# Features of five blocks: rows normed on ScalarE and turned by way of DRAM and VectorE

## The chip, the cores and the metric

The kernel runs on one core of one Trainium2 chip. Times are device microseconds of one execution, as median of the runs shown. A profile is one execution, recorded instruction by instruction; "us" in its timelines counts from its first instruction. The engines have short names there: PE is TensorE, PEld its weight loads, DVE is VectorE, ACT is ScalarE, POOL is GpSimd, SP is SyncE, which here only issues DMAs (SPq).

## The reference, cut to what matters

The kernel computes one layer: a graph step over a dense 4096x4096 adjacency matrix, then attention and a mixture of experts. The change concerns the graph step alone.

```python
def _layernorm(x, axis=-1, eps=1e-5):
    m = jnp.mean(x, axis=axis, keepdims=True)
    v = jnp.var(x, axis=axis, keepdims=True)
    return (x - m) / jnp.sqrt(v + eps)

def _L0_gnn_ref(features, adj, neigh_W, lin_W):
    h = features @ neigh_W.T
    deg = adj.sum(axis=1, keepdims=True) + 1.0
    h = adj @ h / deg
    z = jnp.concatenate([features, h], axis=-1) @ lin_W.T
    return z

# x is 4096 x 256, adj 4096 x 4096, float32
x = x + _L0_gnn_ref(_layernorm(x, axis=-1), adj, L0_gnn_neigh_W, L0_gnn_lin_W)
...
```

## The kernel before

**Tiles.** The 4096 rows of x are eight blocks of 512, each held as `res[b]`: 128 partitions, four row tiles `t`, 256 columns. The adjacency matrix is 8x8 blocks of 512x512, 1 MB each, that stream through three buffers; `load(n)` asks for the next but two as soon as a block is done with. One row of eight such blocks is an aggregation, `aggregate(b)`; each block is multiplied in seven products on halves of it (a Strassen scheme) with the normed rows `g[jb]`. `halve(n)` makes the sums of the adjacency block's halves, `halve_x(b)` those of the rows. The part of lin_W that meets the features themselves does not go through the adjacency matrix: `features(b)` multiplies block b's normed rows, with the columns on the partitions, and adds the product to `res[b]`.

**What happens to one block of x.** `scales_x(b)`: mean and variance on VectorE (L159, L161), then on GpSimd the power -1/2 (L165, L166) into `rstd[b]`. `normed_x(b, t)` (L451): VectorE writes (x - mean) * rstd into `g[b]`, four instructions a block. `turned_x(b)` (L437, L439): TensorE transposes `g[b]` in eight 128x128 pieces and ScalarE copies the result into `turned[b]`. `features(b)` (L509, L514): sixteen matmul passes on TensorE and two adds on VectorE; it also norms block b+1. `halve_x(b)` (L463 to L470): one small copy on ScalarE, four operations on VectorE.

**Order.** The schedule is written out by hand: each engine takes its instructions in the order in which the program names them, and semaphores hold an instruction until what it reads is there. Row 0 of the aggregation has all the work on x in it, some blocks ahead. In its step `jb`, after four of the seven products, come `halve(jb + 1)`, `features(jb + 2)`, `halve_x(jb + 2)` and `scales_x(jb + 4)`; at the step's end `turned_x(jb + 3)`, and then the next adjacency load. Step 0 also has `turned_x(2)`, directly after `halve(1)`. Blocks 0 and 1 are done ahead of the loop, and so are the statistics of blocks 2 and 3. Step 3 has `load_rest`, seven DMAs for the attention's weights.

**The other use of the way through DRAM.** From row 1 on, `qkv(b - 1)` handles the finished block b - 1. It norms its rows into `kT[b]` and `vv[b]`, whose own contents come later, with the columns in the order of `in_order`; `leave` (L599) writes them in two DMAs to a scratch tensor in DRAM, `turning`; `fetch` (L611) reads them back in four DMAs, so that each 32x32 square stands with its 32 rows on 32 partitions; `turn` (L621) has VectorE transpose all squares in two instructions. There are two scratch tensors, used in turns.

Of the kernel before, what the change touches and what calls it, by code (L numbers as in the profile page):

```python
# [9 lines left out]
F32 = mybir.dt.float32  # L10
I32 = mybir.dt.int32
SP = mybir.EngineType.SP
AF = mybir.ActivationFunctionType
ALU = mybir.AluOpType
# [3 lines left out]
P = 128  # L18
N = 4096
C = 256  # L20
NB = 8
TB = 4
# [9 lines left out]
Q = HD // 2  # L32
# [34 lines left out]
def fast_kernel(  # L67
# [24 lines left out]
    nc = tc.nc  # L92
# [27 lines left out]
    for e in range(NE):  # L120
# [16 lines left out]
    res = [  # L137
        res_all[:, b * TB * C : (b + 1) * TB * C].rearrange("p (t c) -> p t c", t=TB)
        for b in range(NB)
    ]  # L140
    qT_all = const.tile([P, NB * 2 * 512], F32, name="qT_all")
    qT = [
        qT_all[:, b * 1024 : (b + 1) * 1024].rearrange("p (c i) -> p c i", c=2)
        for b in range(NB)
    ]
    mv = [const.tile([P, TB, 2], F32, name=f"mv{b}") for b in range(NB)]
# [42 lines left out]
    def in_order(x):  # L189
        return x.rearrange("p (g c d) -> p c g d", g=4, c=2)  # L190

    def in_groups(x):
        return x.rearrange("p (c g d) -> p c g d", g=4, c=2)
# [65 lines left out]
    with (  # L259
# [179 lines left out]
                nc.scalar.copy(dst[:, :, cols], tr.rearrange("p c t i -> p c (t i)"))  # L439

        turned = {}

        def scales_x(b, at_a_time=TB):
            for t in range(0, TB, at_a_time):
                some = slice(t, t + at_a_time)
                stats(gx, b, range(TB)[some])
                power(rstd[b][:, some], mv[b][:, some, 1:2], 1.0, EPS_LN)

        def normed_x(b, t):
            i = t // 2 * 2  # L450
            nc.vector.tensor_scalar(  # L451
                g[b][:, i : i + 2, t % 2, :], res[b][:, t, :].rearrange("p (h c) -> p h c", h=2),
                mv[b][:, t, 0:1], rstd[b][:, t], op0=ALU.subtract, op1=ALU.mult,
            )

        def turned_x(b):

            turned[b] = qT[b % 4]
            transposed(lambda t, c: g[b][:, t // 2 * 2 + c, t % 2, :], turned[b])
# [39 lines left out]
            halves_of[n] = m  # L499
        def features(b):  # L500
            fT = turned.pop(b)
            for t in range(TB if b + 1 < NB else 0):
                normed_x(b + 1, t)
            for h in range(2):
                pj = p_pj.tile([P, 2, C], F32, tag="pj", name=f"pf_{b}_{h}")
                for t in range(2):
                    for c in range(2):
                        at = (2 * h + t) * P
                        nc.tensor.matmul(  # L509
                            pj[:, t, :], fT[:, c, at : at + P], l1_sb[:, c, :],  # L510
                            start=(c == 0), stop=(c == 1),
                        )
                x1 = res[b][:, 2 * h : 2 * h + 2, :]
                nc.vector.tensor_add(x1, x1, pj)  # L514
# [52 lines left out]
                ),  # L567
            )

        turning = [tc.dram_tile([512, C], F32, name=f"turning{n}") for n in range(2)]  # L570
        last_z = gs.tile([P, 1024], F32, name="last_z")

        def qkv(b):

            made = {}

            def scales():
                stats(gx, b)
                var = mv[b][:, :, 1:2]
                power(both[b], var, *BOTH)  # L580
                power(rstd[b], var, 1.0, EPS_LN)

            def norm():

                made["h0"] = [
                    t.rearrange("p (t c) -> p t c", t=2)
                    for t in (kT[b], vv[b].rearrange("p t c -> p (t c)"))
                ]
                for t in range(TB):
                    nc.vector.tensor_scalar(  # L590
                        in_order(made["h0"][t // 2][:, t % 2, :]), in_groups(res[b][:, t, :]),
                        mv[b][:, t, 0:1], both[b][:, t], op0=ALU.subtract, op1=ALU.mult,
                    )
                made["ratio"] = ratio(gx, b)

            def leave():

                for n, h0 in enumerate(made.pop("h0")):
                    nc.sync.dma_start(  # L599
                        turning[b % 2][n * 2 * P : (n + 1) * 2 * P].rearrange(  # L600
                            "(t p) c -> p t c", p=P
                        ),
                        h0,
                    )

            def fetch():

                made["z"] = qT_all[:, (b + 1) * 1024 : (b + 2) * 1024] if b + 2 < NB else last_z
                squares = turning[b % 2].rearrange("(m i) (g e) -> g i m e", i=Q, g=4)
                for n in range(4):  # L610
                    nc.sync.dma_start(  # L611
                        made["z"][n * Q : (n + 1) * Q].rearrange("p (m e) -> p m e", e=2 * Q),
                        squares[n],
                    )

            def turn():

                made["hT"] = qT[b]
                z = made.pop("z").rearrange("p (m c d) -> p c m d", c=2, d=Q)
                for c in range(2):  # L620
                    nc.vector.transpose(  # L621
                        qT[b][:, c, :].rearrange("p (m i) -> p m i", i=Q), z[:, c]
                    )

            def values_and_logits():
                for h in range(2):
                    pj = p_tr.tile([P, 2, 2, P], F32, tag="tr", name=f"pv_{b}_{h}")
                    pj = pj.rearrange("p c t i -> p c (t i)")
                    for i in range(2):
                        at = (2 * h + i) * P  # L630
                        for c in range(2):
                            nc.tensor.matmul(  # L632
                                pj[:, i, 0 : NE + P], made["hT"][:, c, at : at + P],
                                wqkv_sb[:, c, QK:], start=(c == 0), stop=(c == 1),
                            )
                    nc.scalar.copy(vv[b][:, 2 * h : 2 * h + 2, :], pj[:, :, NE : NE + P])  # L636
                    for i in range(2):
                        t = 2 * h + i
                        nc.scalar.activation(
                            first_lg[b][:, t, :], pj[:, i, 0:NE], AF.Copy,  # L640
                            scale=made["ratio"][:, t],
                        )

            def turned_heads(ms):
                pjs = [p_pj.tile([P, 512], F32, tag="pj", name=f"pq_{b}_{m}") for m in ms]
                for m, pj in zip(ms, pjs):
                    for c in range(2):
                        nc.tensor.matmul(
                            pj, wqkv_sb[:, c, m * P : (m + 1) * P], made["hT"][:, c, :],
                            start=(c == 0), stop=(c == 1),  # L650
                        )
                for m, pj in zip(ms, pjs):
                    to = kT[b] if m == 2 else qT[b][:, m, :]
                    rot = gx.tile([P, 512], F32, tag="rot", name=f"rot_{b}_{m}", bufs=1)
                    nc.vector.tensor_mul(to, pj, tables[b][:, 0, :])  # L655
                    for n in range(4):
                        nc.scalar.activation(  # L657
                            rot[n * Q : (n + 1) * Q, :], pj[(n ^ 1) * Q : ((n ^ 1) + 1) * Q, :],
                            AF.Copy, scale=1.0 if n % 2 else -1.0,
                        )  # L660
                    nc.gpsimd.tensor_mul(rot, rot, tables[b][:, 1, :])  # L661
                    nc.gpsimd.tensor_add(to, to, rot)

            return [
                [scales, lambda: turn_tables(b)], [norm, leave], [],
                [values_and_logits, lambda: turned_heads((2,))], [lambda: turned_heads((0, 1))],
            ], {
                (2, "end"): [fetch], (2, "loaded"): [lambda: spread_tables(b)],
                (3, "end"): [turn],
            }  # L670
# [23 lines left out]
        features(1)  # L694
        halve_x(1)
        scales_x(3)
        steps = {jb: [] for jb in range(NB)}
        for jb in range(NB):
            for f, b in (
                (halve, jb + 1), (features, jb + 2), (halve_x, jb + 2), (scales_x, jb + 4),  # L700
            ):
                if b < NB or f is halve:
                    steps[jb].append(lambda f=f, b=b: f(b))
            if jb + 3 < NB:
                steps[jb, "end"] = [lambda b=jb + 3: turned_x(b)]
        steps[0].insert(1, lambda: turned_x(2))
        steps[3].append(load_rest)
        for jb, f in ((5, scale_rest), (6, bounds), (6, turn_wo), (7, router_wo)):
# [2 lines left out]
        for b in range(NB):  # L711
            if b:

                steps = {0: behind, (0, "end"): at_end}
# [2102 lines left out]
```

## Time and profile before

| | |
|---|---|
| median of three runs | 1514.38 us (1513.91 to 1514.47) |
| the profiled execution's own time | 1513.4 us |
| its span, first to last instruction | 1511.7 us |
| row 0 of the aggregation, TensorE's first to last matmul in it | 18.7 to about 96 us |
| HBM read and written | 188.15 MB and 30.80 MB |

Busy time in five stretches of the part that matters; columns are the length, then for each engine the busy us and the number of its instructions, the granted TensorE clock, the busy share of the DMA engines and the GB/s that they moved:

```profile
20.00:24.00 4.00, 3.76 (x22) 3.17 (x21) 3.97 (x11) 1.17 (x3) 0.16 (x1) 1.00 1.02 370
24.00:28.00 4.00, 4.00 (x20) 3.54 (x19) 3.90 (x13) 0.00 (x0) 1.53 (x2) 1.00 0.18 54
28.00:32.00 4.00, 4.00 (x24) 3.46 (x23) 3.97 (x10) 1.21 (x3) 0.46 (x1) 1.00 0.25 61
32.00:36.00 4.00, 4.00 (x21) 3.51 (x20) 3.83 (x13) 0.00 (x0) 1.23 (x2) 1.00 0.48 201
36.00:40.00 4.00, 4.00 (x20) 3.51 (x19) 4.00 (x9) 0.00 (x0) 0.77 (x1) 1.00 0.00 0
```

The engines are TensorE, its weight loads, VectorE, ScalarE and GpSimd, in this order. TensorE is busy in all of each stretch but the first, where it waited 0.24 us for a copy by ScalarE; VectorE is hardly less busy; ScalarE has some 1.2 us of work in 8 to 10 us. A busy TensorE is not one at its peak, because the ends of its matmuls are modelled.

### The profile page before, as it was taken

The numbers are of one execution on the slowest core, as the hardware profiler recorded it, in microseconds if no ns is written. First come the engines' busy times: TensorE is split into PE (matmuls) and PEld (weight loads), VectorE is DVE, ScalarE is ACT, GpSimd is POOL, SyncE is SP. The second block draws the span as 40 slices with busy tenths as digits, with TensorE's granted clock in tenths as the row PEclk, the third lists the DMA queues.
The fourth block names the chain that finished last, engine by engine and source line by source line (L and its number), as shares of the span: only waits on it lengthen the run. The fifth ranks groups of instructions, "written<-read, shape, count | busy, mean of one in ns | idle before, by whom it ended". The sixth has DMA issues, their size and how long they took to land. (4 is left out here: it accounts for less than half of the span.)

```text
span 1511.7 us, 28589 instructions
## 1 busy us (share of the span) xinstructions
PE 1498.3 (99%) x10739; PEld 1103.8 (73%) x10739; DVE 1082.8 (72%) x2237; ACT 545.3 (36%) x977; POOL 564.1 (37%) x649
## 2 busy tenths in 40 slices
PE   9999999999999999999999999999999999999997
PEld 7888888888888544444444444358899999999996
DVE  7855665656765577779879879795676877777872
ACT  2102011021020455655656655653222343343341
POOL 2102122121221331364564653551523464554542
PEclk9999999999999999999999999999999999999999
DMA  6435645555556000011010110029977898999965
GB/s 243 133 119 182 193 151 177 168 168 166 165 183 184 5 1 16 29 50 39 30 59 24 38 43 30 29 77 331 260 182 217 261 272 236 269 270 247 271 157 135
DMA packets 124365, 219.51 MB, mean 145 GB/s; under 512 B 77402, under 2 KB 100698, under 8 KB 110586
## 3 DMA queue, kind: packets, MB, share of 16 engines
q1 hardware_dynamic: 110682, 199.35, 41.5%
q0 software_dynamic: 12720, 17.47, 6.4%
q8 instruction: 86, 1.41, 0.4%
q10 hardware_dynamic: 816, 0.79, 0.2%
q14 instruction: 61, 0.50, 0.1%
HBM read 188.15 MB, written 30.80 MB: 145 GB/s over the span
## 5 line engine op out<-in xcount | busy, mean ns | idle before, releaser
L826 PE MATMUL sc<-qT_all,kT 64*64 64x512 f32 (+3 forms) x2304 | 282.2, 557 | 0.5 <-ACT pt_all L834 0.3
L538 PE MATMUL acc<-a,g 128*128 128x256 f32 x1024 | 244.0, 379 | 0.0
L538 PEld LDWEIGHTS acc<-a,g 128*128 128x128 f32 x1024 | 194.1, 190 | 32.1 <-issue 6.7
L826 PEld LDWEIGHTS sc<-qT_all,kT 64*64 64x64 f32 x2304 | 91.2, 133 | 128.5 <-issue 109.4
L834 ACT ACTIVATE pt_all<-sc 128x1024 f32<-128x1024 f32 (+3 forms) x157 | 148.7, 954 | 96.8 <-PE sc L826 91.8
L1908 POOL DMA_INDIRECT acc_dram<-y,late x40 | 63.0, 1575 | 176.6 <-ACT y L1897 113.2
L538 PE MATMUL acc<-more_sums,g 128*128 128x256 f32 x512 | 126.3, 379 | 0.0
L854 DVE TENSOR_TENSOR late<-late,pt_all 128x1024 f32<-128x1024 f32 (+3 forms) x91 | 106.8, 1173 | 24.3 <-POOL pt_all L836 9.6
L538 PEld LDWEIGHTS acc<-more_sums,g 128*128 128x128 f32 x512 | 97.2, 190 | 13.1
L868 PE MATMUL y_first<-pt_all,vv 64*64 64x512 f32 (+3 forms) x448 | 106.7, 554 | 0.0
L661 POOL TENSOR_TENSOR rot<-rot,tables 128x512 f32<-128x512 f32 x21 | 33.8, 1607 | 192.6 <-ACT rot L657 138.4
L1828 PE MATMUL h<-late,qT_all 128*128 128x256 f32 (+1 forms) x616 | 104.0, 327 | 0.3 <-DMA qT_all<-in_w_dram 0.3
L868 PE MATMUL y_second<-pt_all,vv 64*64 64x512 f32 (+3 forms) x436 | 104.2, 555 | 0.0
L1828 PEld LDWEIGHTS h<-late,qT_all 128*128 128x128 f32 x616 | 93.5, 191 | 9.9 <-ACT late L1512 1.1
L636 ACT COPY vv<-pv 128x256 f32<-128x256 f32 x14 | 5.2, 372 | 252.0 <-PE pv L632 144.1
L1110 POOL DMA_INDIRECT lists<-row,slots x64 | 88.8, 1388 | 17.6 <-issue 15.6
L868 PE MATMUL y_third<-pt_all,vv 64*64 64x512 f32 (+3 forms) x372 | 88.7, 555 | 0.0
L1835 DVE TENSOR_TENSOR late<-si,h 128x256 f32<-128x256 f32 (+2 forms) x87 | 39.3, 466 | 64.4 <-ACT si L1834 46.0
L657 ACT ACTIVATE rot<-pq 32x512 f32<-32x512 f32 x84 | 49.4, 588 | 82.6 <-DVE qT_all L655 35.7
L1834 ACT ACTIVATE si<-h 128x256 f32<-128x256 f32 (+2 forms) x87 | 36.0, 417 | 107.3 <-PE h L1828 90.2
L854 DVE TENSOR_TENSOR sum_all<-sum_all,pt_all 128x1024 f32<-128x1024 f32 (+3 forms) x51 | 56.0, 1098 | 15.8 <-POOL pt_all L836 9.5
L834 ACT ACTIVATE late<-sc 128x1024 f32<-128x1024 f32 (+3 forms) x55 | 50.9, 927 | 41.4 <-PE sc L826 37.1
(491 smaller groups left out, 3335.0 us busy)
## 6 DMA issues: line engine op xcount, KB each, us to landing
a<-in_adj_dram SPq DMA_DIRECT2D x64, 1024.0 KB
qT_all<-in_w_dram SPq DMA_DIRECT2D x18, 1408.0 KB
pt_all<-in_w_dram SPq DMA_DIRECT2D x16, 1408.0 KB
res_all<-in_w_dram SPq DMA_DIRECT2D x17, 768.0 KB
pt_all<-in_w_dram SPq DMA_DIRECT2D x16, 768.0 KB
res_all<-in_w_dram SPq DMA_DIRECT2D x8, 1408.0 KB
qT_all<-in_w_dram SPq DMA_DIRECT2D x9, 768.0 KB
late<-lists SPq DMA_DIRECT2D x96, 64.0 KB
```

Source lines behind the costliest of these rows:

```text
L538: nc.tensor.matmul(acc[bank][:, at, :], g[jb][:, right, k, :], m[left][:, k, :], start=(jb == 0 and k == 0 and at == 0), stop=(jb == NB - ...
L657: nc.scalar.activation(rot[n * Q : (n + 1) * Q, :], pj[(n ^ 1) * Q : ((n ^ 1) + 1) * Q, :], AF.Copy, scale=1.0 if n % 2 else -1.0,)
L661: nc.gpsimd.tensor_mul(rot, rot, tables[b][:, 1, :])
L826: nc.tensor.matmul(ps[k * HP : (k + 1) * HP, j, :w], kT[sb][hd, i * P + k * HP : i * P + (k + 1) * HP], qT[b][hd, p, off:], start=True, st ...
L834: nc.scalar.activation(pt[:, :, :w], ps[:, :, :w], AF.Exp, scale=HD ** -0.5)
L854: nc.vector.tensor_add(sums[b, p][:, :, off:], before[:, :, off:], pt[:, :, : 512 - off])
L868: nc.tensor.matmul(accs[b, p][k][hd, off:], vv[sb][some, i, hd], pt[some, j, : 512 - off], start=(s == order_of(b)[0]), stop=(s == order_o ...
L1110: put = nc.gpsimd.indirect_dma_start(out=lists[:, :], out_offset=bass.IndirectOffsetOnAxis(ap=chosen[b][:, k, t, :], axis=0), in_=flats[b] ...
L1828: nc.tensor.matmul(ps[m % 2][:, m // 2 - q, :], w13_sb[:, c, m * P : (m + 1) * P], xT[:, c, :], start=(c == 0), stop=(c == 1),)
L1834: nc.scalar.activation(si[:, 0:both, :], ps[0][:, 0:both, :], AF.Silu)
L1835: nc.vector.tensor_mul(hT[:, q : q + both, :], si[:, 0:both, :], ps[1][:, 0:both, :])
L1908: put = nc.gpsimd.indirect_dma_start(out=(acc_dram if k < NM - LAST else out)[:, :], out_offset=at, in_=y[:, h, :], in_offset=None, comput ...
```

## The change

Blocks 0, 1 and 2 stay as they were (`FIRST = 3`). For blocks 3 to 7 the norming goes from VectorE to ScalarE, which does it twice: once in the column order of the squares, into `kT[b]` and `vv[b]`, and once into `g[b]`, each in four activations with scale `rstd` and bias `less` = -mean * rstd, a small operation on VectorE. TensorE's transposes of these blocks and ScalarE's copies go. In their place the rows are written to DRAM and fetched back as squares, into the parts of `qT_all` that held first weights (those of blocks 4 and 5, in turns), and VectorE turns them into `turned[b]`. The helpers `rows_of`, `left`, `fetched` and `turn_squares` are the former bodies of qkv's `norm`, `leave`, `fetch` and `turn`, which now call them.

Where the new pieces stand: `staged_x(3)` and `left(3)` directly ahead of row 0's loop, and so ahead of step 0's `turned_x(2)`. In step jb `fetched_x(jb + 3)` comes last of the middle's work, `squares_x(jb + 3)` and `staged_x(jb + 4)` at the step's end, `left(jb + 4)` after the adjacency load.

```diff
+        turning = [tc.dram_tile([512, C], F32, name=f"turning{n}") for n in range(2)]
+
+        def rows_of(b):
+            return [
+                t.rearrange("p (t c) -> p t c", t=2)
+                for t in (kT[b], vv[b].rearrange("p t c -> p (t c)"))
+            ]
+
+        def left(b):
+            for n, rows in enumerate(rows_of(b)):
+                nc.sync.dma_start(
+                    turning[b % 2][n * 2 * P : (n + 1) * 2 * P].rearrange(
+                        "(t p) c -> p t c", p=P
+                    ),
+                    rows,
+                )
+
+        def fetched(b, z):
+            squares = turning[b % 2].rearrange("(m i) (g e) -> g i m e", i=Q, g=4)
+            for n in range(4):
+                nc.sync.dma_start(
+                    z[n * Q : (n + 1) * Q].rearrange("p (m e) -> p m e", e=2 * Q), squares[n]
+                )
+
+        def turn_squares(z, dst):
+            z = z.rearrange("p (m c d) -> p c m d", c=2, d=Q)
+            for c in range(2):
+                nc.vector.transpose(dst[:, c, :].rearrange("p (m i) -> p m i", i=Q), z[:, c])
...
+        FIRST = 3
+
+        def staged_x(b):
+
+            less = gx.tile([P, TB, 1], F32, tag="less", name=f"less_{b}", bufs=1)
+            nc.vector.scalar_tensor_tensor(
+                less, mv[b][:, :, 0:1], -1.0, rstd[b], op0=ALU.mult, op1=ALU.mult
+            )
+            staged = rows_of(b)
+            for t in range(TB):
+                nc.scalar.activation(
+                    in_order(staged[t // 2][:, t % 2, :]), in_groups(res[b][:, t, :]),
+                    AF.Identity, bias=less[:, t], scale=rstd[b][:, t],
+                )
+            for t in range(TB):
+                i = t // 2 * 2
+                nc.scalar.activation(
+                    g[b][:, i : i + 2, t % 2, :],
+                    res[b][:, t, :].rearrange("p (h c) -> p h c", h=2),
+                    AF.Identity, bias=less[:, t], scale=rstd[b][:, t],
+                )
+
+        def fetched_x(b):
+            fetched(b, z_of(b))
+
+        def squares_x(b):
+            turned[b] = qT[b % 4]
+            turn_squares(z_of(b), turned[b])
+
+        def z_of(b):
+            return qT_all[:, (4 + b % 2) * 1024 : (5 + b % 2) * 1024]
...
         def features(b):
             fT = turned.pop(b)
-            for t in range(TB if b + 1 < NB else 0):
+            for t in range(TB if b + 1 < FIRST else 0):
                 normed_x(b + 1, t)
...
         scales_x(3)
+        staged_x(3)
+        left(3)
         steps = {jb: [] for jb in range(NB)}
         for jb in range(NB):
...
             if jb + 3 < NB:
-                steps[jb, "end"] = [lambda b=jb + 3: turned_x(b)]
+                steps[jb].append(lambda b=jb + 3: fetched_x(b))
+                steps[jb, "end"] = [lambda b=jb + 3: squares_x(b)]
+            if jb + 4 < NB:
+                steps[jb, "end"].append(lambda b=jb + 4: staged_x(b))
+                steps[jb, "loaded"] = [lambda b=jb + 4: left(b)]
         steps[0].insert(1, lambda: turned_x(2))
```

More of the change, by code (lines that the diff above doesn't have):

```diff
@@ L568, in turn_banks @@
             )
-        turning = [tc.dram_tile([512, C], F32, name=f"turning{n}") for n in range(2)]
         last_z = gs.tile([P, 1024], F32, name="last_z")
@@ L583, in norm @@
             def norm():
[L585 to L588, printed above, removed]
+                h0 = rows_of(b)
                 for t in range(TB):
                     nc.vector.tensor_scalar(
-                        in_order(made["h0"][t // 2][:, t % 2, :]), in_groups(res[b][:, t, :]),
+                        in_order(h0[t // 2][:, t % 2, :]), in_groups(res[b][:, t, :]),
                         mv[b][:, t, 0:1], both[b][:, t], op0=ALU.subtract, op1=ALU.mult,
@@ L596, in leave @@
             def leave():
[L598 to L604, printed above, removed]
+                left(b)
             def fetch():
                 made["z"] = qT_all[:, (b + 1) * 1024 : (b + 2) * 1024] if b + 2 < NB else last_z
[L609 to L614, printed above, removed]
+                fetched(b, made["z"])
             def turn():
                 made["hT"] = qT[b]
[L619 to L623, printed above, removed]
+                turn_squares(made.pop("z"), qT[b])
             def values_and_logits():
```

## The prediction

> **What bounds the kernel now.** I read the page first (shares of busy time), then the order of time of the stage that the change touches (0 to 100 us: row 0 of the aggregation), engine by engine.
>
> ```profile
> PE 1498.3 (99%) x10739; PEld 1103.8 (73%) x10739; DVE 1082.8 (72%) x2237; ACT 545.3 (36%) x977; POOL 564.1 (37%) x649
> ```
>
> TensorE is busy 99% of the span, so all that TensorE waits anywhere is 13 us. A microsecond off its work is a microsecond off the end, and one that it is made to wait is added: no idle time behind absorbs it. The steps of row 0, as TensorE's timeline shows them:
>
> ```profile
> 20.43 1.03 PE L538 MATMUL acc<-qT_all,g 128*128 128x256 f32 x4
> 21.30 1.03 PE L538 MATMUL acc<-a,g 128*128 128x256 f32 x4
> 22.16 1.04 PE L437 MATMUL tr<-ident,g 128*128 128x128 f32 x8
> 23.43 3.72 PE L509 MATMUL pf<-qT_all 128*128 128x256 f32 x16 [0.24 <-ACT qT_all L439]
> ...
> 40.05 1.04 PE L437 MATMUL tr<-ident,g 128*128 128x128 f32 x8
> 40.92 1.89 PE L538 MATMUL acc<-a,g 128*128 128x256 f32 x8
> ...
> 50.42 1.04 PE L437 MATMUL tr<-ident,g 128*128 128x128 f32 x8
> ```
>
> One step lasts 10.37 us (40.05 to 50.42), of which the eight transposes hold 0.87 (40.05 to 40.92). Note the order at 22 us: transposes of block 2, then its features, 0.24 us later, as soon as ScalarE has copied the transposes out. VectorE in the same stretch:
>
> ```profile
> 24.62 1.40 DVE L159 BATCH_NORM_STATS2 st<-res_all 128x6 f32<-128x256 f32 x4
> 25.94 0.36 DVE L161 BATCH_NORM_AGGREGATE mv<-st 128x2 f32<-128x6 f32 x4
> 26.22 0.66 DVE L495 TENSOR_TENSOR more_sums<-a 128x512 f32<-128x512 f32 x1
> ```
>
> These are the statistics of block 3. VectorE works without a gap from 14 to 47 us, so they end at 26.3 and not earlier, three microseconds after TensorE's transposes of block 2. ScalarE is nearly idle there:
>
> ```profile
> 15.47 0.21 ACT L463 COPY g<-ones 128x4 f32<-128x4 f32 x1
> 22.80 1.07 ACT L439 COPY qT_all<-tr 128x512 f32<-128x512 f32 x2 [7.12 <-PE tr L437]
> ```
>
> The road through DRAM exists already, for the rows of qkv; the timelines of SP and of VectorE show one of its seven trips:
>
> ```profile
> 175.50 0.37 SPq L599 DMA_DIRECT2D turning<-vv  x1
> 177.85 1.92 SPq L611 DMA_DIRECT2D qT_all<-turning  x4
> ```
> ```profile
> 182.76 1.30 DVE L621 STREAM_TRANSPOSE qT_all<-qT_all 128x512 f32<-128x512 f32 x2 [4.17 <-DMA qT_all<-turning]
> ```
>
> Issue of the second write to the first fetch: 2.35 us. First fetch to squares in hand: 4.9; over the seven trips 4.1 to 5.35, median 5.04.
>
> [...] the 28 warming transposes (L681) have 476 ns at most, 272 at least, and the last six, after 4 us, 272. [...]
>
> **The change part by part.**
>
> *Removed.* 40 transposes on TensorE, 5 x 0.87 = 4.35 us, and ten copies of 0.59 us on ScalarE. VectorE loses 4 normings a block (20.54 to 21.84: 1.30).
>
> *Added on VectorE.* Two 32x32 transposes of 128x512 (1.25 from start to next start) and one small operation for the bias, `less` (0.16, as the like-sized ratio). Even by work, but `less` waits for GpSimd's power right after the statistics. With VectorE waiting, that took 1.41 us at 12.23 (10.82 to 12.23); beside a working VectorE 2.17 (26.30 to 28.47). I take 1.41; at 2.17 all below is 0.76 later.
>
> *Added on ScalarE.* Eight activations a block with bias and scale per partition. Nearest row: L392 and L1531, 128x256 with one such operand, 499 ns, two in 0.91, so 0.41 apart. [...] estimated 0.50 apart, 0.59 for one. A batch is 7 x 0.50 + 0.59 = 4.1 us; the four that make the rows take 2.1. Lower end 3.4 and 1.75.
>
> *The first wait, and the largest.* In program order the batch of block 3 stands ahead of `turned_x(2)`, which is still on TensorE, with its copies on ScalarE. So ScalarE has the eight activations of block 3 in front of the copies of block 2. `less` of block 3: 26.30 + 1.41 = 27.7, done 27.9. Batch 27.95 to 32.05, first copy done at 32.7, features of block 2 at 32.75 instead of 23.43. TensorE, in order, has nothing else before them: +9.3 us (8.6 with the short batch, 10.1 with the slow power).
>
> *The clock.* TensorE is idle from 23.2 to 32.75, 9.5 us, so it should restart at half speed. Four microseconds of that, as at the start, lose 2.0. [...]
>
> *Block 3's round.* Rows done 30.05, second write issued 30.1, fetch at 32.45, squares at 37.5. VectorE comes to them only after the adds of block 2 (which wait for the late features: 39.1), halving (1.6) and statistics of 4 (1.6): 42.2, done 43.5. TensorE asks for features 3 at 44.3 (features 2 to 38.2 with the slow clock, 12 matmuls at 0.216 = 2.6, 16 at 0.216 = 3.5). No wait.
>
> *Blocks 4 to 7: a ring.* Behind each pair of square transposes on VectorE stands `less` of the next block; it starts ScalarE's rows, these the writes, these the fetch, this the next transposes. One round: signal 0.1 + rows 2.1 + write 2.35 + fetch 5.0 + transposes 1.25 + `less` 0.2 = 11.0 us. A TensorE step is now 10.37 - 0.87 = 9.50. Starting from `less` of 4 at 44.2: squares of 4 turned at 55.1, TensorE asks at 53.8 (+1.3); the next three rounds each cost 11.0 - 9.5 = 1.5 at most, I take 1.5, 1.4, 1.4. Sum 5.6. With a fetch of 4.15 and rows of 1.75 the round is 9.8: 1.2 in all; with 5.35, 7.6 in all.
>
> *SP.* 30 DMAs more (10 writes, 20 fetches). The load of adjacency block 3 now stands behind block 3's fetch and leaves at about 41 instead of 29.8, since its buffer comes free late too; VectorE wants it at 55. At nothing. Writing 2.6 MB and reading it again falls where the DMA share was 0.0 to 0.9 (4 us stretches from 24 to 72 us). `load_rest`'s seven DMAs stand right behind the fetch of block 6: up to 2 us, in the upper end. GpSimd's order is unchanged.
>
> *Sum.* 9.3 + 2.0 + 5.6 - 4.35 = +12.6 us on the profiled execution's 1513.4: 1526.0. That execution is 1.0 under the median of the three runs (1514.38), so 1527.0 for the median. Least 8.6 + 0 + 1.2 - 4.35 = +5.5, most 10.1 + 3.4 + 7.6 - 4.35 = +16.8: 1519.9 to 1531.2.
>
> **Rivals.**
> 1. *The ring fits and the clock holds.* Fetches land in 4.15, no half speed: 9.3 + 1.2 - 4.35 = +6.2, 1520.6. For it: no table spreads queue behind these fetches as they do in qkv's. Against: an adjacency load does.
> 2. *The ring is slower.* Writes, fetches, loads and `load_rest` share SP and the DMA engines; a round of 13 us costs 3.5 x 4: 9.3 + 2.0 + 14 - 4.35 = +21, 1535.4. For it: 256-byte pieces. Against: seven trips of before stay within 1.3 us.
> 3. *Faster: ScalarE is done with the batch in time.* Then only the transposes go: -4.35, 1510.0. It decides at one point: the batch of block 3 (4.1 us) must be over when the first copy is due at 22.8, so `less` must come by 18.7. Against: the statistics that feed it end at 26.3. For it: only ScalarE's idle time (36% busy).
>
> **How the numbers follow.** The forecast has 0.67 (its own range 1522 to 1531), rival 1 0.15, rival 2 0.13, rival 3 0.05. The range 1519.5 to 1532 takes in the bounds and leaves out rival 3 and most of rival 2. No change means within 0.2%, 3 us. All but rival 3 are slower by more: slower 0.94, same 0.01, faster 0.05.
>
> **What would show it.** Right: TensorE stands still for about 9 us after the transposes of block 2, its features released by ScalarE's copies; the matmuls after it are long for some 4 us; waits of 1 to 2 us ahead of features 4 to 7, put down to VectorE's square transposes, themselves waiting for DMA; row 0 ends some 12 us later, and nothing after it changes. Wrong: features of block 2 at 23 to 25 us (rival 3), or ring waits near zero (rival 1) or above 3 us (rival 2). What would make it wrong: a batch cheaper than 3.4 us, or a clock that holds.

## The result, and the profile after

| | before | after |
|---|---|---|
| median | 1514.43 us (1513.91 to 1515.29, 4 runs) | 1532.11 us (1531.08 to 1533.42, 4 runs) |
| span of the profiled execution | 1511.7 us | 1529.5 us |
| mean granted TensorE clock | 0.998 | 0.993 |

The change makes the kernel slower: ratio 1.0119, 95% interval 1.0107 to 1.0131. The forecast was 1527.0, its range 1519.5 to 1532.0; the time lies 0.1 us above the range.

The line of TensorE in the page of the kernel after, to be read beside the one of before:

```profile
PE 1500.2 (98%) x10699; PEld 1102.5 (72%) x10699; DVE 1087.2 (71%) x2232; ACT 560.7 (37%) x1007; POOL 562.5 (37%) x649
```

The 40 transposes are gone (10739 to 10699), and yet TensorE is busy 1.9 us longer, in a span that is 17.8 us longer. A busy time that rises while work is taken away says that some matmuls ran slower. Where the rest went, its timeline after shows (start, duration, then in brackets the idle time ahead of the group and what ended it):

```profile
22.17 1.04 PE L437 MATMUL tr<-ident,g 128*128 128x128 f32 x8
32.48 5.74 PE L569 MATMUL pf<-qT_all 128*128 128x256 f32 x16 [9.27 <-ACT qT_all L439]
...
44.10 3.62 PE L569 MATMUL pf<-qT_all 128*128 128x256 f32 x16
...
53.89 3.79 PE L569 MATMUL pf<-qT_all 128*128 128x256 f32 x16
...
64.97 3.79 PE L569 MATMUL pf<-qT_all 128*128 128x256 f32 x16 [1.26 <-DVE qT_all L469]
...
75.58 3.79 PE L569 MATMUL pf<-qT_all 128*128 128x256 f32 x16 [0.77 <-DVE qT_all L469]
...
89.75 6.10 PE L569 MATMUL pf<-qT_all 128*128 128x256 f32 x16 [4.34 <-DVE qT_all L469]
```

These are the features of blocks 2 to 7. Two waits are large, 9.27 us ahead of block 2 and 4.34 us ahead of block 7, and just behind these two the same sixteen passes take 5.74 and 6.10 us instead of 3.62 to 3.79. ScalarE's timeline after holds the reason of the first wait:

```profile
27.91 1.09 ACT L494 ACTIVATE kT<-res_all,less,rstd 128x256 f32<-128x256 f32 x2 [12.22 <-DVE less L489]
...
29.89 2.06 ACT L500 ACTIVATE g<-res_all,less,rstd 128x256 f32<-128x256 f32 x4
31.86 1.05 ACT L439 COPY qT_all<-tr 128x512 f32<-128x512 f32 x2
```

For 12 us ScalarE stood before the batch of block 3, which needed `less`; the two copies for block 2, whose transposes had been done since 23 us, came behind it. The windows of the kernel after (length, busy us of TensorE, its loads, VectorE, ScalarE, GpSimd, then granted clock, DMA share, GB/s) show the clock and, further down, the DMA engines:

```profile
29.00:32.40 3.40, 0.00 (x0) 0.00 (x0) 1.50 (x3) 3.40 (x9) 0.00 (x0) 0.50 0.46 154
...
34.00:36.00 2.00, 2.00 (x6) 1.60 (x5) 0.00 (x0) 0.00 (x0) 0.00 (x0) 0.50 0.97 178
...
38.00:42.00 4.00, 4.00 (x21) 3.51 (x20) 3.67 (x13) 0.00 (x0) 0.00 (x0) 1.00 0.19 25
...
68.00:70.00 2.00, 2.00 (x11) 1.77 (x10) 1.81 (x4) 1.64 (x5) 0.00 (x0) 1.00 0.55 182
...
78.00:80.00 2.00, 2.00 (x11) 1.77 (x10) 1.99 (x4) 2.00 (x5) 0.00 (x0) 1.00 1.06 348
```

The clock is at half from within the wait until 36.6 us, with TensorE fully busy from 34 to 36. Row 68 is the time of block 6's writes, and the DMA engines are about half busy (0.55); row 78 is that of block 7's, and they are full (1.06; a share can come out a little over 1). SP's timeline after shows what they carry:

```profile
66.62 0.38 SPq L452 DMA_DIRECT2D turning<-kT  x1
67.61 0.36 SPq L452 DMA_DIRECT2D turning<-vv  x1
69.82 1.91 SPq L462 DMA_DIRECT2D qT_all<-turning  x4
71.78 0.49 SPq L327 DMA_DIRECT2D wqkv_sb<-in_wqkv_dram  x1
...
75.97 0.40 SPq L278 DMA_DIRECT2D a<-in_adj_dram  x1
77.22 0.38 SPq L452 DMA_DIRECT2D turning<-kT  x1
78.21 0.37 SPq L452 DMA_DIRECT2D turning<-vv  x1
83.84 1.92 SPq L462 DMA_DIRECT2D qT_all<-turning  x4
```

From the second write to the fetch block 6 takes 2.21 us (67.61 to 69.82), block 7 takes 5.63 (78.21 to 83.84). Between the two stand `load_rest`'s seven DMAs, 71.8 to 75.9, which push the 1 MB adjacency load to 75.97, right in front of block 7's writes.

The sum closes in TensorE's own terms. The starts of the features give the extra time of each step over a step without transposes (9.50 us; 9.70 for the step behind the features of block 2, which took 10.57 before): 9.05 ahead of block 2 (32.48 against 23.43), 1.92 in the step after it, then 0.29, 1.58, 1.11 and 4.67 ahead of blocks 4 to 7; the features of block 7 are 2.48 longer than before; 4.35 are saved. Together +16.75 us, and all that TensorE does after row 0 starts 16.7 us later, to its last group of matmuls (1517.13 against 1500.47). The other 1.1 us of the span are in the scatters of the output after that group, which take between 10.8 and 12.4 us in the kernels shown here, whatever the edit. That start of TensorE's last group, 2.75 us long, is called "the last group" below; where an expectation speaks of the end of TensorE's last matmul, its figures are of this start. The lines of the last two readings, first of the kernel before, then of the kernel after:

```profile
75.49 3.62 PE L509 MATMUL pf<-qT_all 128*128 128x256 f32 x16
...
1500.47 2.75 PE L1882 MATMUL ye_y<-res_all,late 128*128 128x256 f32 x12
```
```profile
1517.13 2.75 PE L1928 MATMUL ye_y<-res_all,late 128*128 128x256 f32 x12
```

### The profile page after: what moved, and what is told of

Its sections match the earlier page's. It is cut to its first block, busy times and chain, and to the rows that moved or that the text cites. A ratio compares the mean times of both kernels' runs of the same rounds, so it can differ in the third digit from the quotient of the medians.

```text
span 1529.5 us, 28582 instructions
## 1 busy us (share of the span) xinstructions
PE 1500.2 (98%) x10699; PEld 1102.5 (72%) x10699; DVE 1087.2 (71%) x2232; ACT 560.7 (37%) x1007; POOL 562.5 (37%) x649
## 3 DMA queue, kind: packets, MB, share of 16 engines
q8 instruction: 86, 1.41, 0.4%
## 4 chain that ended last, share of the span: by engine, by line
PE 92%; DMA 3%; DVE 2%; ACT 1%; issue 1%; POOL 1%; SPq 0%; DVEq 0%; POOLq 0%
PE acc L598 23%; PE sc L872 15%; PE h L1874 13%; PE y_first L914 5%; PE y_second L914 5%; PE y_third L914 4%; PE ye_y L1928 4%; PE hA L1691 4%; PE ye_y L1831 3%; PE ye_ms L1831 2%; PE pq L688 2%; PE hD L1691 2%; PE ph L199 2%; PE po L994 1%; PE hB L1691 1%; DMA qT_all<-turning 1%
## 5 line engine op out<-in xcount | busy, mean ns | idle before, releaser
L598 PEld LDWEIGHTS acc<-a,g 128*128 128x128 f32 x1024 | 194.4, 190 | 32.4 <-issue 6.7
L872 PEld LDWEIGHTS sc<-qT_all,kT 64*64 64x64 f32 x2304 | 91.1, 133 | 128.6 <-issue 108.7
L701 POOL TENSOR_TENSOR rot<-rot,tables 128x512 f32<-128x512 f32 x21 | 33.3, 1585 | 193.2 <-ACT rot L697 142.6
L1874 PEld LDWEIGHTS h<-late,qT_all 128*128 128x128 f32 x616 | 93.5, 191 | 10.2 <-ACT late L1558 1.3
L880 ACT ACTIVATE late<-sc 128x1024 f32<-128x1024 f32 (+3 forms) x55 | 50.9, 927 | 41.4 <-PE sc L872 36.6
```

The source lines that it names most:

```text
L598: nc.tensor.matmul(acc[bank][:, at, :], g[jb][:, right, k, :], m[left][:, k, :], start=(jb == 0 and k == 0 and at == 0), stop=(jb == NB - ...
L872: nc.tensor.matmul(ps[k * HP : (k + 1) * HP, j, :w], kT[sb][hd, i * P + k * HP : i * P + (k + 1) * HP], qT[b][hd, p, off:], start=True, st ...
L880: nc.scalar.activation(pt[:, :, :w], ps[:, :, :w], AF.Exp, scale=HD ** -0.5)
L1874: nc.tensor.matmul(ps[m % 2][:, m // 2 - q, :], w13_sb[:, c, m * P : (m + 1) * P], xT[:, c, :], start=(c == 0), stop=(c == 1),)
```

## The experiments

Each kernel is compared with runs of the kernel before on the same chip (medians 1513.55 to 1513.92).

**What makes block 7 late: `load_rest` one step later.**

```diff
-        steps[3].append(load_rest)
+        steps[4].append(load_rest)
```

> load_rest's seven DMAs go from step 3 to step 4, behind the fetch of block 7. Theory: they stood ahead of the adjacency load and of the writes of block 7 on SP and on the DMA engines, so its round took 14.2 us instead of 10.7; now it takes 10.5 to 11.5, the wait before features 7 falls from 4.5 to 0.5 to 1.5 us, too short for the clock to go down, so features 7 take 3.8 instead of 6.1: 5 to 6 us less than the changed kernel, 1526 to 1527. Rival (the road through DRAM is slow by itself in that stretch, whatever else is queued): wait 3 us or more, time above 1530.

Measured: 1524.64 us (1523.41 to 1525.27), ratio 1.0071 (1.0054 to 1.0088), the last group 5.5 us earlier than in the changed kernel. SP's and TensorE's timelines of this run:

```profile
72.20 0.42 SPq L278 DMA_DIRECT2D a<-in_adj_dram  x1
77.64 0.38 SPq L452 DMA_DIRECT2D turning<-kT  x1
78.63 0.36 SPq L452 DMA_DIRECT2D turning<-vv  x1
80.88 1.92 SPq L462 DMA_DIRECT2D qT_all<-turning  x4
```
```profile
86.70 3.79 PE L569 MATMUL pf<-qT_all 128*128 128x256 f32 x16 [0.87 <-DVE qT_all L469]
```

The load leaves 5.4 us ahead of the writes instead of 1.25, the fetch comes 2.25 us after the second write, the wait is 0.87, and there is no half clock behind it (features of 3.79 us, a granted clock of 1.00 from 84 to 90 us). One line of the program is worth some 7 us of the median, of which 5.5 are TensorE's and the rest lies in the scatters. It doesn't yet say which of the transfers moved was to blame.

**The writes and the fetch ahead of the adjacency load on SP's queue.**

```diff
             if jb + 3 < NB:
-                steps[jb].append(lambda b=jb + 3: fetched_x(b))
                 steps[jb, "end"] = [lambda b=jb + 3: squares_x(b)]
             if jb + 4 < NB:
-                steps[jb, "end"].append(lambda b=jb + 4: staged_x(b))
-                steps[jb, "loaded"] = [lambda b=jb + 4: left(b)]
+                for f in (staged_x, left, fetched_x):
+                    steps[jb, "end"].append(lambda f=f, b=jb + 4: f(b))
```

(and `fetched_x(3)` behind `left(3)`)

> The changed kernel with one thing moved: on the queue of SP the writes and the fetch of a block stand ahead of the adjacency load of the same step, not behind it; the loads of the table's other tensors stay in step 3. Theory 'the writes wait for the 1 MB load in front of them': for block 7 the fetch starts within 3 us of the issue of the writes (5.6 us in the changed kernel), TensorE waits at most 1.3 us before the features of block 7 and isn't granted half speed there, its last matmul ends 5 to 6.5 us earlier than in the changed kernel (near 1511.5 instead of 1517.1), the time is 1525 to 1527. Rival 'the loads moved in step 3 take SP's time and the DMA engines themselves': the wait before block 7 stays at 3.5 us or more, with half speed after it, and the time stays within 1 us of 1532. A second rival: the adjacency loads, now some 4 to 6 us later, are late themselves, and the sums of VectorE at the start of a step wait for them; then the time is over 1532.

Measured: 1528.25 us (1526.91 to 1528.62), ratio 1.0091 (1.0077 to 1.0105); the last group 2.5 us earlier. The fetch comes 3.0 us after the second write of block 7, TensorE waits 2.69 us, and it does fall to half speed (5.17 us for the features, a granted clock of 0.50 from 87.7 to 91.1). Neither theory's numbers: the adjacency load of this step now leaves at 71.96, 5.9 us ahead of the writes, farther than the 5.4 that cost nothing in the run above; `load_rest`'s loads (778 KB in all) are what stands between, from 72.4 to 76.9, and the writes are delayed by them as well, by less. So it needn't be an adjacency load. The second rival is half right. VectorE's timeline of this run:

```profile
56.83 0.69 DVE L555 TENSOR_TENSOR more_sums<-a 128x512 f32<-128x512 f32 x1 [2.54 <-DMA a<-in_adj_dram]
```

Four times VectorE now waits for an adjacency load, 1.57 to 2.83 us, as it never does in the changed kernel; but it has that time: TensorE's waits for blocks 5 and 6 are 1.19 and 0.92, together what they were (1.26 and 0.77).

**A queue of their own: order in the queue, or the DMA engines?** The writes and fetches of x on ScalarE's queue, once in the changed kernel, once in the later version for blocks 5 to 7 (below). Those of qkv stay on SP's queue.

```diff
-        def left(b):
+        def left(b, queue=nc.scalar):
...
-                nc.sync.dma_start(
+                queue.dma_start(
...
-        def fetched(b, z):
+        def fetched(b, z, queue=nc.scalar):
...
-                nc.sync.dma_start(
+                queue.dma_start(
...
```

> The changed kernel with one thing moved: the writes and fetches of the squares of x are issued on ScalarE's DMA queue, at the same places of the program, so that neither the 1 MB adjacency load nor the loads of step 3 stand in front of them in a queue[...]. Theory 'order in the queue': the fetch of block 7 starts within 3 us of the issue of its writes (5.6 us in the changed kernel), TensorE waits at most 1.3 us before the features of block 7 and keeps full speed there, its last matmul ends near 1511 (1517.1), the time is 1524 to 1527. Rival 'the DMA engines are busy with the load': the fetch comes 5 us or more after the writes, the wait stays at 3.5 us or more, and the time within 1 us of 1532. Putting the writes ahead of one load on SP's queue shortened the time from writes to fetch only to 4.3 us, with the loads of step 3 in front of them instead, and left a wait of 2.7 us: both theories allow that.

> The version for blocks 5 to 7 with the statistics first from step 1 on, and the writes and fetches on ScalarE's DMA queue. Theory 'order in the queue': the fetch starts 2 to 2.6 us after the writes for each of the three blocks (5.0, 6.9 and 7.1 us on SP's queue), the one wait of 0.9 us before the features of block 7 goes, TensorE's last matmul ends near 1498.0, the time is near 1510.5. Rival 'the DMA engines': 5 us or more, and the time stays at 1511 to 1512.

Measured: 1531.41 us (1530.66 to 1535.38), ratio 1.0125 (1.0109 to 1.014), and 1520.48 us (1519.51 to 1522.15), ratio 1.0046 (1.0032 to 1.006); the latter had 1512.07 with its writes on SP's queue. The second answers the question. SP's timeline of the version on SP's queue, and ScalarE's of the one on ScalarE's, for block 6:

```profile
50.93 0.38 SPq L452 DMA_DIRECT2D turning<-kT  x1
51.56 0.36 SPq L452 DMA_DIRECT2D turning<-vv  x1
57.84 1.91 SPq L462 DMA_DIRECT2D qT_all<-turning  x4
```
```profile
50.85 0.38 ACTq L452 DMA_DIRECT2D turning<-kT  x1
...
51.83 0.38 ACTq L452 DMA_DIRECT2D turning<-vv  x1
...
57.89 3.73 ACTq L462 DMA_DIRECT2D qT_all<-turning  x4
```

In both, SP issues an adjacency load at 50.5. On another queue the fetch starts 0.05 us later than on the same one (57.89 and 57.84); for block 5 it is 47.72 in both. So standing behind the load in one queue is not what delays the writes. That leaves the rival, the DMA engines busy with the load. That both queues use the same ones is my estimate: in the changed kernel they were full (1.06 from 78 to 80 us) when block 7's writes were late, and in the first of the two runs they were full while a fetch on ScalarE's queue was slow (below). How they share out their time between two queues was not shown. My theory of the queue, for which the two runs were made, is wrong.

The queue has a price of its own. In this version ScalarE issues the fetch of block 6 at 57.89 and begins the rows of block 7 at 61.99 us, behind 8.14 us without work, whose end its timeline puts down to the fetch. On SP's queue the rows begin at 60.3, an estimate: there the first write of block 7 is issued at 61.43, and for block 6 of this version it is issued 1.13 us after the rows begin (49.72 to 50.85).

The first run also shows what the shared queue had been good for. Without fetches to wait for, SP issues the load and `load_rest` earlier, from 59.7 to 66.1, into block 5's fetch. Its ScalarE and TensorE timelines:

```profile
58.31 8.32 ACTq L462 DMA_DIRECT2D qT_all<-turning  x4
```
```profile
70.45 6.62 PE L569 MATMUL pf<-qT_all 128*128 128x256 f32 x16 [7.32 <-DVE qT_all L469]
```

Four DMAs that are issued in 1.9 us elsewhere take 8.3, while the share of the DMA engines is 0.91, 1.03, 1.07 and 1.16 in the four stretches of 2 us from 60 to 68; VectorE has the squares 11.3 us after the first (5 elsewhere), and TensorE waits 7.32 us for block 5, while block 7 waits 0.32. The total stays: a delay moved, not removed, and that the time is the one which the rival named is a coincidence. The version for blocks 5 to 7 fares alike: `load_rest`, from 60.3 to 66.8, runs into its fetch of block 6, for which TensorE waits 6.25 us and then has half speed (a granted clock of 0.50 from 67.5 to 74.3 us). Neither theory had this in its numbers, and it is why that time is 1520.5 and not 1511: the wait and 2.2 us of half speed, less the 0.86 us that block 7 no longer waits, make the 7.6 us by which its last group is later (1506.31 against 1498.71).

**The clock: matmuls in the first wait.** Twenty matmuls whose result is overwritten go into the bank of the features of block 2, ahead of them.

```diff
                 pj = p_pj.tile([P, 2, C], F32, tag="pj", name=f"pf_{b}_{h}")
+                for n in range(20 if (b, h) == (2, 0) else 0):
+                    nc.tensor.matmul(
+                        pj[:, 0, :], l1_sb[:, 0, 0:P], l1_sb[:, 0, :], start=True, stop=True
+                    )
```

> 20 extra matmuls (40 passes) are put into TensorE's queue ahead of the features of block 2; their results are overwritten. They end at about 31.9 us, before the copies come at 32.5. If the features of block 2 are slow after the first wait because the clock has gone down (theory), they take 3.6 us instead of 5.7 and start at 32.5 as before; the granted clock in 32 to 38 us is 1.00; features of block 3 start at about 42, and all is some 2 us shorter than the changed kernel (1530) unless the later rounds give it back. If they are slow because the second copy or VectorE's adds hold them (rival), they still take 5.7 us and the time stays 1532.

Measured: 1529.59 us (1528.52 to 1530.38), ratio 1.0105 (1.0089 to 1.0122), last group 1.8 us earlier. TensorE's timeline of it:

```profile
32.52 3.72 PE L573 MATMUL pf<-qT_all 128*128 128x256 f32 x16 [0.64 <-ACT qT_all L439]
```

The features start when they did (32.48) and take 3.72 us instead of 5.74, and the mean granted clock of the run is 0.997 (0.993 in the changed kernel): the 2.02 us are the clock's, and the first wait is ScalarE's alone.

**The first wait: block 2's copies ahead of block 3's batch.**

```diff
-        staged_x(3)
-        left(3)
...
+        steps[0].insert(2, lambda: (staged_x(3), left(3)))
```

> The batch of block 3 and its writes are named after the transposes of block 2, so ScalarE's copies come first. Theory: features of block 2 start at 23.4 us and the 9.05 us wait is gone, but block 3's way through DRAM starts only at 29 us (VectorE's small operation for the bias behind the first halving) and gives squares at about 38.5, turned at 39.8; TensorE asks for features 3 at 33.1, so 6 to 7 us of wait and a lower clock (about 2 us) move there. Net 1.5 to 3 us less than the changed kernel (1529 to 1530.5). Rival (the first wait was the only loss before block 7): features 3 wait under 2 us, the time is some 9 us less (1523). Third: the copies weren't what held features 2: they still start at 32.

Measured: 1526.61 us (1525.4 to 1527.42), ratio 1.0083 (1.0066 to 1.01), last group 3.6 us earlier. Block 2 is in time (features at 23.57, waiting 0.24), but TensorE's next features are not:

```profile
39.38 6.15 PE L569 MATMUL pf<-qT_all 128*128 128x256 f32 x16 [6.04 <-DVE qT_all L469]
```

The wait moved one block on. TensorE asks for block 3 at 33.3 us, its statistics end at 26.4, GpSimd's power takes 1.4 at least, and the way through `less`, ScalarE, DRAM and VectorE another 11 us. The order on ScalarE decided which block waits; by these sums, that one must wait comes from starting the detour with block 3.

**A shorter ring: `less` on GpSimd**, right behind the power, so that VectorE's squares don't stand in front of it.

```diff
-            nc.vector.scalar_tensor_tensor(
-                less, mv[b][:, :, 0:1], -1.0, rstd[b], op0=ALU.mult, op1=ALU.mult
-            )
+            nc.gpsimd.tensor_tensor(less, mv[b][:, :, 0:1], rstd[b], op=ALU.mult)
+            nc.gpsimd.tensor_scalar(less, less, -1.0, 0.0, op0=ALU.mult, op1=ALU.add)
```

> The bias is made by two small GpSimd operations after its power instead of one on VectorE behind the square transposes of the block before, so the ring is cut: ScalarE's rows start when the statistics are done. Theory (the ring through VectorE sets the rounds of blocks 5 to 7): the waits before features 5 and 6 (1.4 and 0.9 us) fall to under 0.5; the first wait stays at 9.1 (half a microsecond longer by the second operation); block 7 keeps its wait to a large part, since load_rest stands ahead of it. 1 to 3 us less than the changed kernel. Rival (writes and fetches alone set the rounds): the waits stay within 0.3 us of the changed kernel.

Measured: 1531.3 us (1530.56 to 1532.83), ratio 1.0116 (1.0099 to 1.0133), last group 1.3 us later: a miss. The first wait grows to 10.67, blocks 4 and 5 wait 1.16 and 1.08, block 6's wait goes, block 7's is 3.75, with 6.70 us for the features behind it. In their steps the rows are ready earlier, but then the writes come sooner behind a load, 4.2, 3.9 and 1.0 us for blocks 5 to 7 (5.2, 5.4 and 1.25 in the changed kernel), and the fetch follows the second write after 2.8 to 5.5 us.

**Fewer blocks by this way.** `less` on GpSimd, `load_rest` in step 4, the statistics ahead of the adds in each step, and the way through DRAM from block 4 or from block 5 on, the blocks below keeping their transposes. A control has the kernel before with two of these edits alone: `load_rest` in step 4 and the early statistics.

```diff
-        FIRST = 3
+        FIRST = 5
...
-                (halve, jb + 1), (features, jb + 2), (halve_x, jb + 2), (scales_x, jb + 4),
+                (halve, jb + 1), (scales_x, jb + 4), (features, jb + 2), (halve_x, jb + 2),
```

> All found so far together: the way through DRAM begins with block 4 (FIRST = 4), the bias comes from GpSimd, the statistics of block jb + 4 are taken before the adds of block jb + 2 instead of after them, load_rest stands behind the fetch of block 7. If the order is all that costs (theory), each block's rows start some 4 us earlier against TensorE's steps, the waits before features 4 to 7 are under 0.5 us each, and the four transposes saved (3.5 us) come through: row 0 ends 2.5 to 3.5 us before that of the kernel before, 1511 to 1512. If the road is too long whatever the order (rival), waits of 1 us and more stay at each of the four blocks and the time is 1514 or more.

> As the kernel before it, with the way through DRAM from block 5 on only: one more step of lead for the first round. Theory: no wait before features 5 to 7 at all, 3 x 0.87 = 2.6 us less than the kernel before, 1512. Rival: 1514 or more.

> The kernel before with only the two moves of order (statistics ahead of the adds, load_rest in step 4) and no way through DRAM. TensorE does not wait in row 0 of the kernel before, so both theories expect no change: 1513.5 to 1515. If it is faster by 1 us or more, a gain of the other two is not the way's.

Measured: from block 4 on 1517.07 us (ratio 1.0024, 1.0014 to 1.0034), from block 5 on 1513.91 (1.0003, 0.9995 to 1.0012), control 1514.98 (1.001, 1.0004 to 1.0017). The first wait is gone, and with it both half clocks: the features take 3.62 to 3.79 us. From block 4 on, blocks 5 to 7 wait 1.47, 1.39 and 1.53 us: now their writes start 0.5 to 0.7 us behind a load, and the fetch comes 7.3 to 8.1 us after the second write. From block 5 on, block 6 alone waits, 0.36 us. The control shows what the early statistics cost: in step 0 they put the norming of block 3 behind them, and TensorE's transposes of block 3 wait 1.22 us for it.

So step 0 went back to the old order in three more versions: from block 5 on; the same with the writes and fetch ahead of the load; and that from block 4 on.

> The version in which ScalarE norms blocks 5 to 7 alone, with the statistics ahead of the adds only from step 1 on (step 0 in the order of the kernel before). If the statistics in step 0 alone cost the 1.2 us wait before the transposes of block 3, that wait goes, TensorE's last matmul ends near 1498.4 (1499.6 with them) and the time is near 1512.7. If the wait only moves to another place, the time stays at 1513.9.

> As the version for blocks 5 to 7, and the writes and the fetch of a block ahead of the adjacency load of the step. Theory 'the writes wait for the load in front of them': the fetch starts 2 to 2.6 us after the issue of the writes (4.1 to 6.6 behind the load), no features wait, TensorE's last matmul ends near 1498.1, the time is near 1512.4. Rival: the time from write to fetch doesn't change with the order, and neither does the time (1512.7 to 1513.9).

> The same for blocks 4 to 7. With the loads in front, blocks 5 to 7 waited 1.4 to 1.5 us each. Theory 'the writes wait for the load in front of them': those waits go, four transposes at 0.87 us are saved, TensorE's last matmul ends near 1497.3 (1503.3 with the loads in front and the statistics first in step 0), the time is near 1511.6. Rival 'the round itself is too long, whatever the order on SP': waits of about 1 us before the features of blocks 5 to 7 stay, and the time is 1514 or more.

| version | median us | ratio to before, 95% | last group | waits of features |
|---|---|---|---|---|
| from block 5 on | 1512.07 | 0.999 (0.9984 to 0.9997) | 1498.71 | block 7: 0.86 |
| from 5, writes ahead | 1510.78 | 0.9979 (0.9969 to 0.9989) | 1499.06 | 6: 0.84, 7: 0.44 |
| from 4, writes ahead | 1517.67 | 1.0024 (1.0015 to 1.0033) | 1503.85 | 4: 4.02, with half clock (0.50 from 45.9 to 52.7 us) |

The wait in step 0 is gone, and two versions end ahead of the kernel before, by 0.1% and 0.2%. Which of these two is better isn't shown: the second has the lower median and the later last group. The kernel before with only their order of the statistics was not run, but the gain is accounted for: the transposes of three blocks, 2.6 us, less the waits in the table leave 1.75 and 1.33 us, and the last group is 1.76 and 1.41 us earlier than before. Putting the writes ahead of one load put those of block 6 behind the previous one (load at 48.40, writes at 50.65 and 51.63, fetch at 57.79), so the expected 2 to 2.6 us didn't come, and VectorE waits for the later loads here too, up to 3.54 us. From block 4 on, the statistics of block 4 now come last in step 0, its rows leave at 38.7, and block 4 is late as block 3 was in the run with block 2's copies first: a miss that I could have read from the forecast's own 11 us.

## Why the prediction was right and wrong

*The first wait* held: +9.3 forecast, +9.05 measured, by the forecast's cause. `less` came at 27.71 (27.7), the batch at 27.91 (27.95), and the first copy was done at 32.4 (32.7). The 0.50 us from one activation to the next and the 0.59 for one were my estimate, not shown by the profile of before, whose rows with one such operand have 0.41 and 0.499 us; it is met: four in 2.06 us.

*The clock* held: +2.0 forecast, 1.92 in the sum above, and 2.02 off the features in the run that kept TensorE busy. That half speed follows the wait is shown (9.27 us of wait, a granted clock of 0.50 from 26.37 to 36.61); that it cost just 2.0 is partly luck. What it could cost at most the profile of before did not show: the 3.4 in the forecast's sum was my estimate. Behind the same wait the features of block 2 took 6.42 us in the run with `load_rest` one step later and 5.17 with ScalarE's queue, against 3.72 at full speed: 2.7 and 1.45 lost.

*Block 3's round*: no wait, as forecast (44.10; 44.3).

*The ring* held as a mechanism and for three of its four rounds. From `less` to `less` they last 10.7, 11.1 and 10.6 us (11.0 forecast), and cost 0.29, 1.58 and 1.11 (1.3, 1.5 and 1.4).

*The step that failed* is the term for block 7, the last 1.4 of "1.5, 1.4, 1.4", and with it "`load_rest`'s seven DMAs stand right behind the fetch of block 6: up to 2 us, in the upper end". I had seen the seven DMAs and priced their issue on SP, and these 2 us stand in none of the sums: the most of +16.8 has 7.6 for the ring, which is four rounds with the slow fetch (7.4, not 7.6) and nothing else. With them the upper end would have been some 1533 us, above what was measured. But the size was not the main thing. What the seven DMAs did was to hold back the adjacency load until 1.25 us ahead of block 7's writes, so that the writes went through DMA engines that were full (1.06 from 78 to 80 us). The term measured 4.67, and the 4.3 us of waiting cost the clock a second time, 2.48: 7.15 in place of 1.4. That alone is +5.75; the ring's other rounds gave back 1.2, first wait and clock 0.3. So TensorE's part is +16.75 in place of +12.6, and 1.1 us in the scatters behind it, of which no run showed the cause, bring the 17.8. That the time still came out only 0.1 us above the range, less than its runs differ among themselves, is no sign that the mechanism for block 7 was nearly right. Rival 2 named the resource (the DMA engines), but as an even 3.5 us in each of four rounds; it hit one round.

*The bound of half speed* was too narrow in kind: the forecast asked for the clock only at the first wait, and the wait of 4.34 us ahead of block 7 brought a granted clock of 0.50 as well (87.81 to 94.64).

*Rivals 1 and 3* fall: the ring's waits were not near zero, and the features of block 2 came at 32.5, not at 23.4.

## What to carry to other kernels

A detour through DRAM has a length, here 10.6 to 11.1 us from bias to squares when nothing is in its way; start it only with the first block whose deadline is that far off, here block 5, and count the engines that must all be free on the way. For each write whose landing is waited for, look at what the DMA engines carry in the 5 us before it, on any queue: a 1 MB load issued 1 to 2.5 us ahead of the second write made 2.2 us from it to the fetch into 5 to 8. And when a step on a queue is delayed, follow the bulk transfer behind it to what it will collide with, then price each wait twice, as time and as clock.

## What the runs showed of the hardware

**The clock keeps its own grid.** The granted clock was 0.50 for 3.4, 6.8 or 10.2 us at a time, in twelve stretches of eight of the kernels (the one at each kernel's end left out). In the kernel after it fell at 26.37 and rose at 36.61 (10.24), fell at 87.81 and rose at 94.64 (6.83), and the two falls are 61.44 us apart: 3, 2 and 18 times 3.413, the third part of 10.24. Three other runs show two stretches: their falls are 61.44 us apart with the writes ahead of the load, 37.55 in the changed kernel with ScalarE's queue and 47.79 with block 2's copies first, 18, 11 and 14 times 3.413. A short wait was enough for one fall: in the run with the writes ahead of the load TensorE stood still for 2.69 us only, from 85.40 on. In the 3.41 us that ended with the fall (84.28 to 87.69) it had been busy for a third, and half speed came all the same. Waits up to 1.53 us (from block 4 on) were followed by features of 3.79 us, at full speed. What a wait of 3.75 us or more lost behind it lay between 1.5 and 2.9 us, and the length of the wait doesn't tell which: 1.5 behind 4.58 us (the run with the twenty matmuls, 5.30 us for the features instead of 3.79), 2.8 behind 4.28 (block 2's copies first, 6.63). What differs is where the wait met the grid: in these two runs the next rise of the clock came 3.28 and 5.95 us after the features had begun, and about half of that is lost.

**A separate queue did not separate.** The fetch started 2.1 to 2.7 us after the second of the two writes of 256 KB when the last adjacency load had left 6 us or more before it and none of `load_rest`'s loads stood between. When the second write followed a 1 MB load within 3.6 us, the fetch started 7.2 to 9.4 us after the issue of the load, and to within 0.05 us at the same time from SP's and from ScalarE's queue (47.72 and 47.72, 57.84 and 57.89). In the changed kernel with ScalarE's queue the four DMAs of block 5's fetch, the first issued at 58.31 us, took 8.32 us to issue, beside the 1 MB that SP had asked for at 59.71 and `load_rest`'s loads behind it on SP's queue, 60.09 to 66.1; the fetches of blocks 4, 6 and 7 in the same run took 1.95.
